# A grouped cosine transform on TensorE: from 64x64 tiles in two turns to sixteen 32x32 tiles, placed in front of the side work

## The chip, the core and the metric

The kernel runs on one core of a Trainium2 chip. A core has a matrix engine (TensorE, PE in the profile, its weight loads shown apart as PEld), VectorE (DVE), ScalarE (ACT), GpSimd (POOL), and SyncE (SP), which here only issues DMAs. Each engine works through its own instructions in order; semaphores tie them together. DMA engines, sixteen for this core, move data between device memory and the on-chip memory of 128 partitions. TensorE writes into PSUM, eight banks of 2 KB per partition.

The metric is the device time of one execution in microseconds (us). Three runs of the kernel before gave 6804.09, 6806.48 and 6808.73 us.

## What is computed

Layer 0 is a block-matching network on x of shape (8, 32, 128, 128), normalised per group; layer 1 is a 5x5 convolution. Cut to what matters:

```python
xb = _patch_match_stack(x)            # for each pixel the 8 best offsets: 32*8 = 256 channels, c*8 + k
dct = _conv(xb, dct_w, groups=C)      # 1x1, 32 groups of 8 channels -> 8 channels each
h = relu(_conv(_conv(xb, w1), w2, groups=CK, pad=1))
h = relu(_conv(_conv(h, w3), w4, groups=CK, pad=1))
wiener = sigmoid(_conv(_conv(h, w5), w6, groups=CK, pad=1))
filt = _conv(wiener * dct, inv_dct_w, groups=C)
x = x + _conv(filt, agg_w)            # layer 0, on the normalised x
x = x + _conv5x5(_gn(x), kernel)      # layer 1
```

The change concerns the second line, the cosine transform: a 256x256 matrix that is zero outside 32 blocks of 8x8.

## The kernel before, in words

An image is worked through in 16 row blocks of 8 rows (`NS`), and one more step that flushes the last rows: 17 steps for each of 8 images, 136 in all. The main loop runs over these steps and one slot for each stage, `i` in (3, 2, 1, 0), the stages being skewed against each other. In slots 3, 2 and 1 a 1x1 convolution (`pointwise_v` L649, `pointwise_t` L673) and a depthwise 3x3 run: half the channels on DVE in nine taps (`depthwise_v`, L703, the first tap on ACT at L700), half on PE (`depthwise_t`, L729). Every slot also gathers pixels for a later row block by one-hot matmuls (`gather_pixels`, L611, tile pg). Slot 0 finishes a row block: `final_dct` multiplies the network's output acc by the cosine transform, and in the next slot `final_add` (L809, L817) mixes down to 32 channels.

What other images need (patch distances, top-8, layer 1 of the previous image) is side work: generators that queue pieces for DVE ("D"), ACT ("A") and PE ("P" and "Q"), taken up by `run` at fixed places in each slot. Pieces of "P" are transposes (px, pt, pi), small statistics (pm, pv_a, pv_b) and the 5x5 convolution (two tiles p, L902). The order on PE, DVE and ACT is the program's order; DMAs are issued from POOL and SP.

PSUM: almost all matmul results go through one pool of five banks (`ps_x`): pv, p, pg, pc, pa, px, pt, pi and the rest. A new tile gets a bank once its earlier tile has been read by ACT or DVE. Two further banks belong to the depthwise stage, one to the patch distances.

The transform's way through memory: pixels are gathered into xb (partition 32j + c, second index g, for channel c*8 + 4g + j), which serves as input of the first convolution and is written to device memory as xbd by one DMA for each row block (L620), in the same layout. A step later `final_load` (L769) reads rows shifted by 3 back as xf, eight DMAs of 32 partitions. xf has a single buffer, so its next load waits for the matmuls that read it. `final_dct` then runs twice, for four rows each: two tiles pc (one for each half of the channels), four 64x64 matmuls of fp32 with up to 512 columns into them, and two DVE products L796. The weights ldct are built once in `mixes`: 32 small DMAs on SP into dq (L291), one reduction and two products on DVE.

In slot 0 the order on PE is: side work "P", final_dct, side work "Q", then pg.

Of the kernel before, what the change touches and what calls it, by code (L numbers as in the profile page):

```python
# [8 lines left out]
F32 = mybir.dt.float32  # L9
# [6 lines left out]
P = 128  # L16
C, K, H, W = 32, 8, 128, 128
CK = C * K
NO = 25
R = 8  # L20
# [14 lines left out]
C_M32 = C_G2 + 32  # L35
# [7 lines left out]
def bm3d_conv_preact(  # L43
# [16 lines left out]
    nc = tc.nc  # L60
    NB = x.shape[0]

    const = ctx.enter_context(tc.tile_pool(name="const", bufs=1))
    keep = ctx.enter_context(tc.tile_pool(name="keep", bufs=1))
    xnp = ctx.enter_context(tc.tile_pool(name="xn", bufs=1))
    work = ctx.enter_context(tc.tile_pool(name="work", bufs=2))
    dram = ctx.enter_context(
        tc.tile_pool(name="dram", bufs=2, space=bass.MemoryType.DRAM)
    )
    ps_x = ctx.enter_context(  # L70
        tc.tile_pool(name="ps_x", bufs=5, space=bass.MemoryType.PSUM)
    )
# [23 lines left out]
    cst = const.tile([P, C_N], F32, name="cst")  # L96
# [5 lines left out]
    lw5 = const.tile([P, 2, CK], F32, name="lw5")  # L102


    ldct = const.tile([P, 2, 64], F32, name="ldct")
    lagg = const.tile([P, 2, C], F32, name="lagg")


# [92 lines left out]
    def run(which, credit=1e9):  # L201

        q, took = queues[which], 0.0
        for _ in range(len(q) if which != "D" else 1000):

            i = next(
                (
                    i
                    for i, (c, _, at) in enumerate(q)
                    if at <= now[0] and (c != PAIR or pairs[0] < 2)  # L210
                ),
                None,
            )
            if i is None or took >= credit:
                break
            cost, task, _ = q[i]
            del q[i]
            took += cost
            pairs[0] += cost == PAIR
            push(task)  # L220
        if which == "Q":
            pairs[0] = 0
        return took
# [58 lines left out]

    def mixes():

        dq = work.tile([P, 2, K], F32, name="dq", tag="dq", bufs=1)
        src = dct_w.rearrange("(m h c i) k a b -> m h k c (i a b)", m=2, h=2, i=K)
        for k in range(K):
            for m in range(2):
                for h in range(2):
                    p = 64 * h + 8 * k  # L290
                    nc.sync.dma_start(dq[p : p + 8, m], src[m, (h + m + 1) % 2, k])  # L291
        m8 = work.tile([P, 8], F32, name="m8", tag="m16", bufs=1)
        yield "D", 1.0, 10
        nc.vector.tensor_reduce(
            m8,
            cst[:, C_M32 : C_M32 + C].rearrange("p (a c) -> p c a", c=8),
            axis=mybir.AxisListType.X,
            op=ALU.add,
        )
        for m in range(2):  # L300
            nc.vector.tensor_tensor(
                ldct[:, m].rearrange("p (c i) -> p c i", i=K),
                m8.unsqueeze(2).to_broadcast([P, 8, K]),
                dq[:, m].unsqueeze(1).to_broadcast([P, 8, K]),
                ALU.mult,
            )

        iv = work.tile([P, 2, K], F32, name="iv", tag="iv", bufs=1)
        nc.sync.dma_start(iv, inv_w.rearrange("(m p) k a b -> p m (k a b)", p=P))
        ag = work.tile([C, CK], F32, name="ag", tag="xr")  # L310
        nc.sync.dma_start(ag, agg_w.rearrange("c i a b -> c (i a b)"))
        for m in range(2):
            yield "D", 0.5
            ib = work.tile([P, P], F32, name=f"ib_{m}", tag="xm")
            nc.vector.tensor_tensor(
                ib.rearrange("p (c k) -> p c k", k=K),
                cst[:, C_M16 : C_M16 + 16].unsqueeze(2).to_broadcast([P, 16, K]),
                iv[:, m].unsqueeze(1).to_broadcast([P, 16, K]),
                ALU.mult,
            )  # L320
            yield "P", 0
            ps = ps_x.tile([P, 512], F32, name=f"ps_ag_{m}", tag="x")[:, :C]
            nc.tensor.transpose(ps, ag[:, m * P : (m + 1) * P], ident[:C, :C])
            agt = work.tile([P, C], F32, name=f"agt_{m}", tag="agt")
            nc.scalar.copy(agt, ps)
            yield "P", 0
            ps2 = ps_x.tile([P, 512], F32, name=f"ps_ia_{m}", tag="x")[:, :C]
            nc.tensor.matmul(ps2, ib, agt, start=True, stop=True)
            nc.scalar.copy(lagg[:, m], ps2)
# [270 lines left out]
    def gather_pixels(b, s4, g):  # L600

        n, h = s4 // 2, s4 % 2
        if h == 0 and g == 0:
            xbs[b, n] = xbp.tile([P, 2, R, W], F32, name=f"xb_{b}_{n}", tag="xb")
        xb, xt = xbs[b, n], xts[b, s4]
        sels = [selss.pop((b, s4, g, k2)) for k2 in range(2)]
        pg = ps_x.tile([P, 4, W], F32, name=f"pg_{b}_{s4}_{g}", tag="x")
        for t in range(NT):
            xa, xz = TW * t, min(TW * (t + 1), W)
            for j in range(4):  # L610
                nc.tensor.matmul(  # L611
                    pg[C * j : C * (j + 1), :, xa:xz],
                    xt[:, t],
                    sels[j // 2][:, j % 2, :, xa:xz],
                    start=True,
                    stop=True,
                )
        nc.scalar.copy(xb[:, g, 4 * h : 4 * h + 4], pg)
        if h == 1 and g == 1:
            nc.gpsimd.dma_start(xbd[b][:, :, R * n : R * (n + 1)], xb)  # L620

# [124 lines left out]
    def final_load(b, n):  # L748
        j0, j1 = (3, R) if n == 0 else (0, R if n < NS else 3)
        ya, yz = R * n - 3 + j0, R * n - 3 + j1  # L750

        whole = j1 - j0 == R
        nr, nw = (2, W) if whole else (j1 - j0, C)
        xr = work.tile([P, 2 * W], F32, name=f"xr_{b}_{n}", tag="xr")
        xr = xr[:, : nr * nw].rearrange("p (r w) -> p r w", w=nw)
        for j in range(4):
            ra = ya + 2 * j if whole else ya
            xa = 0 if whole else C * j
            nc.gpsimd.dma_start(
                xr[C * j : C * (j + 1)], x[b, :, ra : ra + nr, xa : xa + nw]  # L760
            )

        xf = xbp.tile([P, 2, R, W], F32, name=f"xf_{b}_{n}", tag="xf", bufs=1)
        src = xbd[b].rearrange("(j m h c) g y x -> g m h j c y x", j=4, m=2, h=2)
        for m in range(2):
            for h in range(2):
                for g in range(2):
                    p = 64 * h + C * g
                    nc.gpsimd.dma_start(  # L769
                        xf[p : p + C, m, j0:j1], src[g, m, (h + m + 1) % 2, :, :, ya:yz]  # L770
                    )
        return xr, xf, j0, j1

    def final_dct(b, n, acc, xf, j0, j1):

        for r0 in range(0, R, 4):
            a, z = max(r0, j0), min(r0 + 4, j1)
            if a >= z:
                continue


            pc = [
                ps_x.tile([P, 4, W], F32, name=f"pc_{b}_{n}_{m}_{r0}", tag="x") for m in range(2)
            ]
            for h in range(2):
                for m in range(2):
                    o = 64 * ((h + m + 1) % 2)
                    nc.tensor.matmul(  # L788
                        pc[m][o : o + 64, : z - a],
                        ldct[64 * h : 64 * h + 64, m],  # L790
                        xf[64 * h : 64 * h + 64, m, a:z],
                        start=True,
                        stop=True,
                    )
            for m in range(2):
                nc.vector.tensor_mul(acc[m][:, a:z], acc[m][:, a:z], pc[m][:, : z - a])  # L796

    def final_add(b, n, acc, xr, j0, j1):

# [213 lines left out]
    with tc.manual_schedule(engines=ORDERED):  # L1013
        push(prep(0))
        push(weights())
        push(mixes())
        xbd[0] = dram.tile([P, 2, H, W], F32, name="xbd_0", tag="xbd")
        for i in range(3):
            nc.gpsimd.memset(tb[i][0:64, :, 0], 0.0)
        for u in range(7):  # L1020
# [12 lines left out]
        for s in range(len(steps) + 2):  # L1033
            if s < len(steps):
                b, n = steps[s]
                if s == 2:
                    push(bands())
                if n == (0 if b else 4) and b + 1 < NB:
                    until(lambda: b in ready, 4.0)
                    push(prep(b + 1))  # L1040
                if n == NS - 1 and b + 1 < NB:
                    until(lambda: b + 1 in ready, 4.0)
                    xbd[b + 1] = dram.tile([P, 2, H, W], F32, name=f"xbd_{b+1}", tag="xbd")
            for i in (3, 2, 1, 0):
                si = s - (i - 1 if i else 2)
                live = 0 <= si < len(steps)
# [10 lines left out]
                if live and not i:  # L1057
# [1 line left out]
                        x1d[bi] = dram.tile([C, H, W], F32, name=f"x1d_{bi}", tag="x1d")  # L1059
                        stats[bi] = work.tile([P, NS + 1, 6], F32, name=f"stat_{bi}", tag="stat")  # L1060
                    xr, xf, j0, j1 = fins.pop(si)
                run("P")
                if live and not i:
                    final_dct(bi, ni, accs[3, bi, ni], xf, j0, j1)

                run("Q")
                if s < len(steps):
                    unit(gather_select, u + 1, (0,))
# [87 lines left out]
```

## Time and profile before

| | |
|---|---|
| median of 3 runs | 6806.48 us |
| span of the profiled execution | 6807.3 us |
| mean granted TensorE clock | 0.973 |
| pc matmuls, L788 | 2112 records, median 589 ns |
| products L796 on DVE | 528, median 681 ns |
| idle of PE and its weight loads ahead of pc, until DVE's L796 | 93.6 us |
| idle of DVE until PE's pc | 59.8 us |
| xf loads on POOL, L769 | 1088 issues, 650.2 us busy; median 7.1 us to landing |
| xbd writes on POOL, L620 | 128 issues, median 732 ns |
| dq loads on SP, L291 | 32 issues, 661 to 870 ns |

The span is that of one execution taken by the hardware profiler. A line of a view by groups gives line, engine, operation, result<-inputs with shapes, count, then busy time and mean duration, then idle time of the engine just before, with what ended it (the releaser). In the view by time each row is a start, a duration, and the merged instructions of one kind; a bracket gives the idle time before it. The records of a matmul overlap: one of 512 columns lasts 589 ns, but tiles side by side start a few ns apart and the next round starts when the array is free. An fp32 matmul has two records.

### The profile page before, as it was taken

The numbers are of one execution on the slowest core, as the hardware profiler recorded it, in microseconds if no ns is written. First come the engines' busy times: TensorE is split into PE (matmuls) and PEld (weight loads), VectorE is DVE, ScalarE is ACT, GpSimd is POOL, SyncE is SP. The second block draws the span as 40 slices with busy tenths as digits, with TensorE's granted clock in tenths as the row PEclk, the third lists the DMA queues.
The fourth block names the chain that finished last, engine by engine and source line by source line (L and its number), as shares of the span: only waits on it lengthen the run. The fifth ranks groups of instructions, "written<-read, shape, count | busy, mean of one in ns | idle before, by whom it ended". The sixth has DMA issues, their size and how long they took to land.

```text
span 6807.3 us, 257036 instructions
## 1 busy us (share of the span) xinstructions
PE 6354.3 (93%) x113378; PEld 3352.8 (49%) x113378; DVE 5860.4 (86%) x8822; ACT 5064.6 (74%) x6698; POOL 3246.7 (48%) x5351
## 2 busy tenths in 40 slices
PE   5798899999999999999999999999999999999997
PEld 1454454554545455454554455545555454455553
DVE  7789988989889898898988888899888899877776
ACT  5787778777687777877777777877769777687772
POOL 7354446444464444544445444454436554344334
PEclk8899999999999999999999999999999999999998
DMA  4566656666566675666756656566665666566653
GB/s 90 143 153 153 151 149 154 159 152 158 147 156 155 144 169 135 163 151 152 167 135 158 161 146 169 138 165 159 149 150 151 162 156 152 138 170 157 154 151 80
DMA packets 809627, 1021.41 MB, mean 150 GB/s; under 512 B 255456, under 2 KB 619936, under 8 KB 808512
## 3 DMA queue, kind: packets, MB, share of 16 engines
q0 software_dynamic: 422432, 745.61, 42.9%
q1 hardware_dynamic: 383568, 258.11, 17.4%
q8 instruction: 892, 14.61, 0.9%
q10 hardware_dynamic: 2512, 1.25, 0.1%
q14 instruction: 223, 1.83, 0.1%
HBM read 553.25 MB, written 217.01 MB: 113 GB/s over the span
## 4 chain that ended last, share of the span: by engine, by line
PE 55%; DVE 23%; ACT 8%; DMA 6%; issue 5%; POOL 3%; SPq 0%; ACTq 0%; DVEq 0%; POOLq 0%
PE pw L729 18%; DVE acc L703 15%; PE pv L649 13%; PE p L673 12%; PE pg L611 4%; DVE df L421 3%; PE pc L788 2%; DMA t<-t 2%; PE p L902 2%; ACT df L429 2%; ACT ib L596 2%; DVE idx L514 1%; PE pa L809 1%; DMA xf<-xbd 1%; DVE acc L796 1%
## 5 line engine op out<-in xcount | busy, mean ns | idle before, releaser
L703 DVE SCALAR_TENSOR_TENSOR acc<-tv,dwv,acc 128x1024 f32<-128x1024 f32 (+3 forms) x3264 | 4032.9, 1237 | 249.6 <-ACT acc L700 140.3
L729 PE MATMUL pw<-t,dwd 96*32 96x254 f32 (+7 forms) x31680 | 2144.1, 422 | 84.7 <-issue 40.5
L729 PEld LDWEIGHTS pw<-t,dwd 96*32 96x32 f32 (+1 forms) x31680 | 1103.9, 111 | 906.6 <-issue 440.7
L582 POOL DMA_DIRECT2D ib<-idxd x1024 | 570.7, 558 | 1796.5 <-ACT sel L597 1620.6
L596 ACT ACTIVATE ib<-ib,nplace 128x1024 bf16<-128x1024 bf16 x1024 | 1170.1, 1143 | 9.5 <-DMA ib<-idxd 9.5
L597 ACT ACTIVATE sel<-ib 128x1024 f32<-128x1024 bf16 x1024 | 1084.8, 1059 | 32.5
L673 PE MATMUL p<-acc,lw 128*32 128x256 f32 x16768 | 989.1, 381 | 25.3 <-ACT tv L657 22.7
L649 PE MATMUL pv<-acc,lw 128*128 128x512 f32 (+1 forms) x2112 | 980.7, 607 | 29.9 <-DVE acc L796 27.4
L769 POOL DMA_DIRECT2D xf<-xbd x1088 | 650.2, 630 | 304.2 <-PE pc L788 87.0
L673 PEld LDWEIGHTS p<-acc,lw 128*32 128x32 f32 x16768 | 556.2, 111 | 454.9 <-ACT tv L657 62.5
L657 ACT COPY tv<-pv 128x512 f32<-128x512 f32 (+2 forms) x784 | 438.1, 578 | 390.4 <-PE pv L649 374.2
L611 PEld LDWEIGHTS pg<-sel,xt 128*32 128x32 f32 x45056 | 575.5, 111 | 252.1 <-issue 54.2
L429 ACT ACTIVATE df<-df 128x786 f32<-128x786 f32 (+2 forms) x576 | 468.0, 859 | 291.9 <-DVE df L421 289.2
L611 PE MATMUL pg<-sel,xt 128*32 128x48 f32 x45056 | 592.7, 207 | 80.4 <-ACT sel L597 46.0
L421 DVE TENSOR_TENSOR df<-xn 128x786 f32<-128x786 f32 (+2 forms) x576 | 532.5, 976 | 116.0 <-PE pd L436 109.2
L742 ACT ACTIVATE acc<-pw 128x512 f32<-128x512 f32 (+2 forms) x808 | 439.9, 573 | 249.7 <-PE pw L729 249.0
L649 PEld LDWEIGHTS pv<-acc,lw 128*128 128x128 f32 x2112 | 384.2, 193 | 475.6 <-issue 398.1
L707 ACT ACTIVATE acc<-acc 128x1024 f32<-128x1024 f32 (+3 forms) x408 | 416.8, 1022 | 229.7 <-DVE acc L703 229.5
L680 ACT COPY t<-p 128x512 f32<-128x512 f32 x800 | 424.6, 570 | 127.7 <-PE p L673 125.7
L700 ACT ACTIVATE acc<-tv,dwv 128x1024 f32<-128x1024 f32 (+3 forms) x408 | 454.5, 1114 | 52.6 <-PE pa L809 35.0
L649 PE MATMUL pv<-xb,lw 128*128 128x512 f32 x1024 | 477.4, 609 | 0.0
L673 PE MATMUL p<-xb,lw 128*32 128x256 f32 x8192 | 468.1, 380 | 4.4 <-DVE xy L914 4.4
(151 smaller groups left out, 5782.5 us busy)
## 6 DMA issues: line engine op xcount, KB each, us to landing
ib<-idxd POOLq DMA_DIRECT2D x1024, 256.0 KB, 4.4
xbd<-xb POOLq DMA_DIRECT2D x128, 1024.0 KB, 6.7
xf<-xbd POOLq DMA_DIRECT2D x960, 128.0 KB, 7.3
t<-t SPq DMA_DIRECT2D x792, 128.0 KB
t<-t SPq DMA_DIRECT2D x384, 256.0 KB
tv<-tv SPq DMA_DIRECT2D x384, 130.0 KB
xt<-xtd POOLq DMA_DIRECT2D x240, 176.0 KB, 4.6
xl<-xs POOLq DMA_DIRECT2D x256, 64.0 KB, 2.6
```

Source lines behind the costliest of these rows:

```text
L421: nc.vector.tensor_sub(df[:, :, ca:cz], xn[:, r0 : r0 + SR, ca:cz], xn[:, r0 + dy : r0 + dy + SR, ca + dx : cz + dx],)
L429: nc.scalar.activation(df[:, :, ca:cz], df[:, :, ca:cz], AF.Square)
L582: nc.gpsimd.dma_start(ib.rearrange("p k y x -> p (k y x)"), idxd[b][s4 // 8, s4 % 8, 4 * k0 : 4 * k0 + 8] .rearrange("k x -> (k x)") .part ...
L596: nc.scalar.activation(ib, ib, AF.Square, bias=nplace)
L597: nc.scalar.activation(sel, ib, AF.Relu, scale=-1.0, bias=1.0)
L611: nc.tensor.matmul(pg[C * j : C * (j + 1), :, xa:xz], xt[:, t], sels[j // 2][:, j % 2, :, xa:xz], start=True, stop=True,)
L649: nc.tensor.matmul(ps[:, :hr], lhsT[:, g, P:CK], src(g)[:, h : h + hr], start=g == 0, stop=g == 1,)
L673: nc.tensor.matmul(ps[C * r : C * (r + 1), e, :nb], lhsT[:, g, s], rows[:, r : r + 4 * nb - 3 : 4], start=g == 0, stop=g == 1,)
L700: nc.scalar.activation(acc, rows, AF.Copy, scale=tap)
L703: nc.vector.scalar_tensor_tensor(acc, rows, tap, acc, op0=ALU.mult, op1=ALU.add)
L729: nc.tensor.matmul(pt[u][C * j : C * (j + 1), ka:kz, :nb, xa:xz], dwd[0:hi, i - 1, u, j, dx + 1], t[0:hi, j, ka:kz, :nb, xa + dx : xz + dx ...
L769: nc.gpsimd.dma_start(xf[p : p + C, m, j0:j1], src[g, m, (h + m + 1) % 2, :, :, ya:yz])
```

## The change

The transform is cut into 32x32 tiles. The channels go to xbd in natural order (c*8 + k), so that 32 consecutive channels are four whole blocks of 8; xbd is written by four DMAs in place of one. xf is loaded for s = 0 to 3 (channel half s // 2, rows 4 (s % 2) and on) with the partitions rotated by 32 s, in one or two DMAs each: seven for a full step instead of eight. `final_dct` takes four pc tiles at once and issues sixteen 32x32 matmuls: row group q of the array writes column group (q + s) % 4 of tile s, so that all sixteen lie on different tiles of the array. Then come four products. ldct has four parts instead of two, dq is loaded by 64 DMAs instead of 32, and DVE does four products in `mixes` instead of two. In the main loop final_dct moves ahead of `run("P")`.

```diff
-        for k in range(K):
-            for m in range(2):
-                for h in range(2):
-                    p = 64 * h + 8 * k
-                    nc.sync.dma_start(dq[p : p + 8, m], src[m, (h + m + 1) % 2, k])
+        src = dct_w.rearrange("(m q c i) k a b -> m q c k (i a b)", m=2, q=4, i=K)
+        for s in range(4):
+            for q in range(4):
+                for c in range(4):
+                    p = C * q + K * c
+                    nc.sync.dma_start(dq[p : p + K, s], src[s // 2, (q + s) % 4, c])
...
-            nc.gpsimd.dma_start(xbd[b][:, :, R * n : R * (n + 1)], xb)
+            for j in range(4):
+                nc.gpsimd.dma_start(
+                    xbd[b].rearrange("(c g j) y x -> j c g y x", g=2, j=4)[
+                        j, :, :, R * n : R * (n + 1)
+                    ],
+                    xb[C * j : C * (j + 1)],
+                )
...
-        for m in range(2):
-            for h in range(2):
-                for g in range(2):
-                    p = 64 * h + C * g
+        src = xbd[b].rearrange("(m p) y x -> m p y x", m=2)
+        for s in range(4):
+            m, r0 = s // 2, s % 2 * 4
+            a, z = max(r0, j0), min(r0 + 4, j1)
+            for pa, pz, at in ((0, P - C * s, C * s), (P - C * s, P, 0)):
+                if a < z and pa < pz:
                     nc.gpsimd.dma_start(
-                        xf[p : p + C, m, j0:j1], src[g, m, (h + m + 1) % 2, :, :, ya:yz]
+                        xf[pa:pz, m, a:z],
+                        src[m, at : at + pz - pa, R * n - 3 + a : R * n - 3 + z],
                     )
...
+        parts = [(s, max(s % 2 * 4, j0), min(s % 2 * 4 + 4, j1)) for s in range(4)]
+        parts = [(s, a, z) for s, a, z in parts if a < z]
+        pc = {
+            s: ps_x.tile([P, 4, W], F32, name=f"pc_{b}_{n}_{s}", tag="x") for s, a, z in parts
+        }
+        for q in range(4):
+            for s, a, z in parts:
+                o = C * ((q + s) % 4)
+                nc.tensor.matmul(
+                    pc[s][o : o + C, : z - a],
+                    ldct[C * q : C * (q + 1), s],
+                    xf[C * q : C * (q + 1), s // 2, a:z],
+                    start=True,
+                    stop=True,
+                )
+        for s, a, z in parts:
+            m = s // 2
+            nc.vector.tensor_mul(acc[m][:, a:z], acc[m][:, a:z], pc[s][:, : z - a])
...
-                run("P")
                 if live and not i:
                     final_dct(bi, ni, accs[3, bi, ni], xf, j0, j1)
-
+                run("P")
                 run("Q")
```

More of the change, by code (lines that the diff above doesn't have):

```diff
@@ L102, in bm3d_conv_preact @@
     lw5 = const.tile([P, 2, CK], F32, name="lw5")
-    ldct = const.tile([P, 2, 64], F32, name="ldct")
+    ldct = const.tile([P, 4, C], F32, name="ldct")
     lagg = const.tile([P, 2, C], F32, name="lagg")
@@ L283, in mixes @@
     def mixes():
-        dq = work.tile([P, 2, K], F32, name="dq", tag="dq", bufs=1)
-        src = dct_w.rearrange("(m h c i) k a b -> m h k c (i a b)", m=2, h=2, i=K)
-        for k in range(K):
-            for m in range(2):
-                for h in range(2):
-                    p = 64 * h + 8 * k
-                    nc.sync.dma_start(dq[p : p + 8, m], src[m, (h + m + 1) % 2, k])
-        m8 = work.tile([P, 8], F32, name="m8", tag="m16", bufs=1)
+        dq = work.tile([P, 4, K], F32, name="dq", tag="dq", bufs=1)
+        src = dct_w.rearrange("(m q c i) k a b -> m q c k (i a b)", m=2, q=4, i=K)
[4 more added lines that the diff above has]
+                    nc.sync.dma_start(dq[p : p + K, s], src[s // 2, (q + s) % 4, c])
+        m4 = work.tile([P, 4], F32, name="m4", tag="m16", bufs=1)
         yield "D", 1.0, 10
         nc.vector.tensor_reduce(
-            m8,
-            cst[:, C_M32 : C_M32 + C].rearrange("p (a c) -> p c a", c=8),
+            m4,
+            cst[:, C_M32 : C_M32 + C].rearrange("p (a c) -> p a c", a=4),
             axis=mybir.AxisListType.X,
@@ L299, in mixes @@
         )
-        for m in range(2):
+        for s in range(4):
             nc.vector.tensor_tensor(
-                ldct[:, m].rearrange("p (c i) -> p c i", i=K),
-                m8.unsqueeze(2).to_broadcast([P, 8, K]),
-                dq[:, m].unsqueeze(1).to_broadcast([P, 8, K]),
+                ldct[:, s].rearrange("p (c i) -> p c i", i=K),
+                m4.unsqueeze(2).to_broadcast([P, 4, K]),
+                dq[:, s].unsqueeze(1).to_broadcast([P, 4, K]),
                 ALU.mult,
@@ L763, in final_load @@
         xf = xbp.tile([P, 2, R, W], F32, name=f"xf_{b}_{n}", tag="xf", bufs=1)
-        src = xbd[b].rearrange("(j m h c) g y x -> g m h j c y x", j=4, m=2, h=2)
-        for m in range(2):
-            for h in range(2):
-                for g in range(2):
-                    p = 64 * h + C * g
+        src = xbd[b].rearrange("(m p) y x -> m p y x", m=2)
+        for s in range(4):
+            m, r0 = s // 2, s % 2 * 4
+            a, z = max(r0, j0), min(r0 + 4, j1)
+            for pa, pz, at in ((0, P - C * s, C * s), (P - C * s, P, 0)):
+                if a < z and pa < pz:
                     nc.gpsimd.dma_start(
-                        xf[p : p + C, m, j0:j1], src[g, m, (h + m + 1) % 2, :, :, ya:yz]
+                        xf[pa:pz, m, a:z],
+                        src[m, at : at + pz - pa, R * n - 3 + a : R * n - 3 + z],
                     )
@@ L774, in final_dct @@
     def final_dct(b, n, acc, xf, j0, j1):
[L776 to L796, printed above, removed]
+        parts = [(s, max(s % 2 * 4, j0), min(s % 2 * 4 + 4, j1)) for s in range(4)]
[16 more added lines that the diff above has]
+            nc.vector.tensor_mul(acc[m][:, a:z], acc[m][:, a:z], pc[s][:, : z - a])
     def final_add(b, n, acc, xr, j0, j1):
@@ L1016, in bm3d_conv_preact @@
         push(mixes())
-        xbd[0] = dram.tile([P, 2, H, W], F32, name="xbd_0", tag="xbd")
+        xbd[0] = dram.tile([CK, H, W], F32, name="xbd_0", tag="xbd")
         for i in range(3):
@@ L1042, in bm3d_conv_preact @@
                     until(lambda: b + 1 in ready, 4.0)
-                    xbd[b + 1] = dram.tile([P, 2, H, W], F32, name=f"xbd_{b+1}", tag="xbd")
+                    xbd[b + 1] = dram.tile([CK, H, W], F32, name=f"xbd_{b+1}", tag="xbd")
             for i in (3, 2, 1, 0):
```

## The prediction, made before the changed kernel was run

> **What bounds the kernel now.** I read the page's parts first: engine shares, then the chain that ended last.
>
> ```profile
> PE 6354.3 (93%) x113378; PEld 3352.8 (49%) x113378; DVE 5860.4 (86%) x8822; ACT 5064.6 (74%) x6698; POOL 3246.7 (48%) x5351
> ...
> PE 55%; DVE 23%; ACT 8%; DMA 6%; issue 5%; POOL 3%; SPq 0%; ACTq 0%; DVEq 0%; POOLq 0%
> ```
>
> TensorE bounds more than half of the span, VectorE about a quarter, and they take turns: stretches in which PE never idles alternate with stretches in which the nine-tap depthwise on DVE (L703) ends last. So a saving on PE counts in the first kind and vanishes in the second. The whole chain, piece by piece, holds 165 us of "PE pc L788" (the page rounds to 2%). I went through the 136 groups of pc (one per row step) in order of time. 92 stand without side work just before them; in 56 of those the chain runs through the whole group (1.88 us). In the others the chain is on DVE.
>
> A plain group, PE's rows in order of time (start, duration, engine, line, operation, count):
>
> ```profile
> 3054.75 1.06 PE L729 MATMUL pw<-t,dwd 128*32 128x508 f32 x8
> 3055.74 1.95 PE L788 MATMUL pc<-xf,ldct 64*64 64x512 f32 x16
> 3057.62 1.12 PE L611 MATMUL pg<-sel,xt 128*32 128x48 f32 x88
> ```
>
> Eight matmuls are 16 records, two passes each. Single records start in fours 7 ns apart, and the fours 0.43 us apart: four rounds of 0.43 plus about 0.17 at the ends is 1.88 us until pg.
>
> A group behind the 5x5 convolution's p (L902), PE and DVE:
>
> ```profile
> 3097.07 10.52 DVE L703 SCALAR_TENSOR_TENSOR acc<-tv,dwv,acc 128x1024 f32<-128x1024 f32 x8
> ...
> 3103.68 4.48 PE L902 MATMUL p<-xm,band 64*64 64x512 f32 x40
> ...
> 3107.98 2.97 PE L788 MATMUL pc<-xf,ldct 64*64 64x512 f32 x16
> ...
> 3109.13 1.28 DVE L796 TENSOR_TENSOR acc<-acc,pc 128x512 f32<-128x512 f32 x2 [1.53 <-PE pc L788]
> 3109.87 0.20 PEld L788 LDWEIGHTS pc<-xf,ldct 64*64 64x64 f32 x6 [0.89 <-DVE acc L796]
> 3110.89 1.01 PEld L611 LDWEIGHTS pg<-sel,xt 128*32 128x32 f32 x88 [0.81 <-DVE acc L796]
> ```
>
> The two p tiles hold two of the five PSUM banks, so the fourth pc waits for the first multiply to give its bank back. From the first p to pg PE needs 7.21 us. DVE's taps end at 3107.59: it is free 3.91 us after p begins.
>
> **1. Sixteen 32x32 tiles.** Two rounds instead of four: 2 x 0.43 + 0.17 + twelve more tiles at 7 ns (0.08) = 1.11 to 1.14 us, a saving of 0.74. No row of this trace has over four tiles at once, so this is the change's largest unknown; the ends are below. Two rules of the Trainium skill bear on it. "TensorE: Matmul & The Clock Gate" (Part 3, what overlaps and what doesn't) says matmuls start in strict program order. In that order a tile's second pass would hold back the next tile's first: eight matmuls would take nine rounds, 3.9 us, and sixteen 17 rounds, 7.3 us. The trace has four rounds, and in the group above one tile's second pass ran while the next tile still waited for DVE, so both passes stand together in the program and the array takes other tiles past a waiting one. "TensorEngine Tiling (Array Packing)" (Gotcha 1) speaks against the change directly: different row tiles can't access one PSUM bank at the same time. Here all four row groups write every pc tile. By that rule they run one after another: 4 x 2 rounds = 3.4 us, 1.7 us worse per group. But today's pc has two row groups writing each bank and runs at full rate, so I take the row, not the rule. Between: a window that passes few waiting tiles gives three rounds (1.45 us, saves 0.43) or five (2.31 us, costs 0.43). I take two rounds, because nothing in the four-tile rows shows a limit. Sum: 56 x 0.74 = 41 us; some stretches will hand part to DVE, so **-38**.
>
> **2. pc in front of the side work.** Four pc tiles are now taken at once, then the side work asks for banks.
> - Behind p5 (the L902 rows; 13 groups, all on the chain): p needs two banks and one is free. Its second tile waits until the first multiply ends: DVE is free at 3.91, plus 0.68 is 4.59, plus 0.07 to wake PE. Then ten rounds less what ran, 4.3 us: pg at 8.97 instead of 7.21. DVE gains its 1.53 and 0.58 of waiting, but PE is the bound there (the next rows wait for PE). 13 x 1.76 = **+23**.
> - First step of an image with px and pv_b (6 groups on the chain): PE stands 6.29 us for the first multiply, then pays pc 1.98, pd 2.7, pg.
>
> ```profile
> 1134.51 1.29 PE L788 MATMUL pc<-xf,ldct 64*64 64x128 f32 x10
> 1142.09 1.98 PE L788 MATMUL pc<-xf,ldct 64*64 64x512 f32 x6 [6.29 <-DVE acc L796]
> ```
>
>   All pc now run before DVE arrives; what waits for the multiply's bank is at worst pv_b (0.28). Saves 1.7 each: **-10**; up to 6 each if pv_b gets another bank.
> - pi+pi (7 groups, in 5 the multiplies come 10.2 us after pi) and pt (8): the next tile takes either the bank of the side tile, freed by an ACT copy within about 1.5 us, or pc's, freed by DVE. With the first, 0. With the second, pg waits for the multiply and pv comes 1.1 + 5.2 us after it instead of at once: 5 x 6.3 = 31 us for pi. For pt ACT's later copy of pv covers it (17.9 us after pt, pv's end by then at most 16). I take **0** and keep 31 as an end; below zero there is nothing, as the multiplies themselves end no earlier.
>
> **3. Setup.** SP's rows and DVE's rows of the setup:
>
> ```profile
> 23.42 22.99 SPq L291 DMA_DIRECT2D dq<-in_L_conv_dct_w_dram  x32
> ...
> 53.24 0.40 DVE L301 TENSOR_TENSOR ldct<-m,dq 128x64 f32<-128x64 f32 x2
> ```
>
> 64 issues of 64 four-byte elements instead of 32: 23.0 us more of SP, dq complete at about 71.5 instead of 48. Today the 6.8 us until 53.24 hide it; then DVE, in order, would stand 18.3 us at L301, with the squares of the first image behind it (iv, ag and kb, queued after dq on SP, arrive by 73 and are not later than that). DVE idles 6.07 us at 78.88 today and is 97% busy in the 30 us after; the delay left there is 72.8 + 18.3 - 78.9 = **+12** (ends 6 and 18). It passes through idxd to the first gather, which starts the pipeline.
>
> **4. POOL and DMA.** xf: 7 issues for 8 (3 for 8 in an image's last step), at 0.6 us; xbd: 4 for 1, about 0.65 each: +1.3 us of POOL per step. POOL is 48% busy and waits 1620.6 us for sel before its ib loads, which cover this; ib waits of ACT are 9.5 us in all. Where dsum or x1d stand behind them: **+4** (0 to 10). xf's packets shrink from 4096 to 2048 bytes: the same DMA kinds took 188 and 98 ns (medians over the trace), 4% more per byte; xf lands a step ahead. Nothing. Two more DVE products at 0.2 us in the setup: nothing.
>
> **Sum** against the profiled run (span 6807.3 us, 0.8 above the 6806.48 median, so the two are interchangeable): -38 + 23 - 10 + 0 + 12 + 4 = -9, **6797 us**, within 0.2% (14 us, about what a measurement tells from no change).
>
> **Rivals.**
> - A (45%): as above, gain and new waits nearly cancel. Own range 6772 to 6822.
> - B (25%): the array doesn't hold sixteen tiles. For it: nothing in the trace exceeds four, and the tiling rule. Against: today's two row groups. Five rounds turn -38 into +25: 6860. Three rounds: 6813. It decides at four rounds.
> - C (18%): banks. After pi the pool hands out pc's bank, and PE stands behind DVE's late multiplies: +31, 6828. For it: PE's 93.6 us of idle at pc already ends on L796. It decides as soon as pi or pg has a wait released by L796 of over 5 us.
> - D (12%): better than A. The gain counts in all plain groups (92 x 0.74 = 68) and pv_b runs early (36): 6807 - 68 - 36 + 23 + 12 = 6738. For it: DVE's waits for pc (59.8 us) go. Against: with DVE late, pv waits for L796 whatever PE does.
>
> **How the numbers follow.** Slower than 6820: all of five rounds (15%), three rounds in half (7%), most of C (16%), A's upper tail (7%): 45%. Faster than 6793: D and A's lower tail, 30%. Between: 25%. The range 6748 to 6860 leaves about 1 in 10 at each end.
>
> **What will show it.** pc x32 records in about 1.2 us, in two rounds (A) or more (B). pg or pi waiting for L796 (C). p of L902 waiting some 3.5 us for L796 in 13 groups. DVE idle 18 us ahead of ldct in the setup, and the first pc 12 us later. I am wrong if pc's group isn't near 1.1 us, if the L902 waits are absent, or if the DVE stretches shift as a whole.

## The result, and the profile after

The changed kernel took 6881.02 us (median of 4 runs, 6877.89 to 6884.7); the kernel before, beside it on the same chip, 6807.6. The ratio is 1.0102, 95% interval 1.0088 to 1.0115: 73 us slower, where 6797 was forecast. A second set of runs on another chip gave 6877.38 against 6801.93, ratio 1.0112 (1.0092 to 1.0132).

The page of the changed kernel, engine shares and the chain that ended last:

```profile
PE 6305.0 (92%) x115490; PEld 3350.9 (49%) x115490; DVE 5861.2 (85%) x8824; ACT 5060.9 (74%) x6698; POOL 3264.3 (47%) x5567
...
PE 44%; DVE 31%; issue 7%; ACT 7%; DMA 7%; POOL 3%; SPq 0%; ACTq 0%; DVEq 0%; POOLq 0%
```

TensorE is busy 49 us less than before, as a smaller transform should make it, and its share of the chain has fallen by 11 points. The time was not saved: it turned into waits. The view of waits, PE alone (us in all, times, longest):

```profile
PE pw L735 <- DMA t<-t: 80.0, 21, 11.1
...
PE pg L611 <- DVE acc L801: 39.4, 10, 7.0
PE pv_b L248 <- DVE acc L801: 39.2, 6, 6.6
PE p L907 <- DVE acc L801: 35.6, 13, 3.5
```

The rows of the same view before:

```profile
PE pc L788 <- DVE acc L796: 38.3, 7, 6.4
...
PE pw L729 <- DMA t<-t: 27.5, 19, 4.4
```

Before, pg waited 3.0 us once for the products, and pv_b and p not at all; the 38.3 us of pc are gone after. (Lines move by a few between kernels: the products are L796 before, L801 here, L805 to L810 in the experiments; the 5x5 part's p is L902, L907, L911.)

Where did the time go? Each row step has four groups of pg; take the start of the first of them in both traces and subtract. Between steps 4 and 5 of images 1 to 6 the difference jumps by 12.2, 12.5, 11.9, 11.1, 10.7 and 11.1 us, and not in image 7. Over every other step it moves by at most 7.4 us, up or down: after the jumps of images 4 and 6 it falls by 7, and over steps 9 to 11, where the 5x5 part stands, it mostly rises. One of these places, PE of the changed kernel in order of time:

```profile
1203.94 2.75 PE L735 MATMUL pw<-t,dwd 96*32 96x256 f32 x46
1217.82 4.52 PE L735 MATMUL pw<-t,dwd 96*32 96x256 f32 x48 [11.13 <-DMA t<-t]
```

Before, the same 94 matmuls ran in one go:

```profile
1195.68 5.33 PE L729 MATMUL pw<-t,dwd 96*32 96x256 f32 x94
```

The second half of pw needs rows of t that SP's queue copies from one group of partitions to another. SP's rows, first before, then after:

```profile
1185.03 0.50 SPq L635 DMA_DIRECT2D tv<-tv  x1
1187.27 0.59 SPq L685 DMA_DIRECT2D t<-t  x1
1187.90 0.94 SPq L687 DMA_DIRECT2D t<-t  x1
1192.25 0.59 SPq L628 DMA_DIRECT2D t<-t  x1
1197.23 0.50 SPq L635 DMA_DIRECT2D tv<-tv  x1
```

```profile
1193.28 12.75 SPq L641 DMA_DIRECT2D tv<-tv  x2
1206.12 0.63 SPq L634 DMA_DIRECT2D t<-t  x1
1206.85 1.10 SPq L691 DMA_DIRECT2D t<-t  x1
1208.00 1.41 SPq L693 DMA_DIRECT2D t<-t  x1
```

Before, the shift of t (L685, L687) goes out between two copies of tv. After, the second tv<-tv stands in front of it, and SP waits 11.67 us in the middle of "x2" for DVE's taps to have read the rows that it overwrites. PE runs out of work at 1206.69. The two parts of the shift go out at 1206.85 and 1208.00, and the second, the one for which PE waits longest, lands 9.7 us after its issue. It lands among other traffic. The next answer gives for a stretch how long PE, PEld, DVE, ACT and POOL were busy, then the granted clock, the busy share of the DMA engines and GB/s; in its first row the DMA engines are 92% busy, with a row block's stores of xbd and its loads of xf.

```profile
1206.00:1218.00 12.00, 0.87 (x18) 0.40 (x12) 11.57 (x34) 3.68 (x5) 5.88 (x11) 0.71 0.92 272
1218.00:1230.00 12.00, 12.00 (x104) 5.15 (x103) 6.36 (x12) 5.24 (x7) 0.00 (x0) 0.86 0.08 20
```

Nothing in the diff writes this order down. `manual_schedule` takes the program's order for PE, DVE and ACT only; SP and POOL are ordered when the program is planned, and the plan came out differently. The orders of the two programs differ in several places; the swap shown, the copy of tv ahead of the shift of t in step 3 of stage 1, stands in images 1 to 6 and in no other: the images with the jumps.

### The profile page after: what moved, and what is told of

The parts are those of the page before. It is cut to its first block, busy times and chain, and to the rows that moved or that the text cites. A ratio compares the mean times of both kernels' runs of the same rounds, so it can differ in the third digit from the quotient of the medians.

```text
span 6876.1 us, 261554 instructions
## 1 busy us (share of the span) xinstructions
PE 6305.0 (92%) x115490; PEld 3350.9 (49%) x115490; DVE 5861.2 (85%) x8824; ACT 5060.9 (74%) x6698; POOL 3264.3 (47%) x5567
## 4 chain that ended last, share of the span: by engine, by line
PE 44%; DVE 31%; issue 7%; ACT 7%; DMA 7%; POOL 3%; SPq 0%; ACTq 0%; DVEq 0%; POOLq 0%
DVE acc L709 23%; PE pw L735 15%; PE pv L655 12%; PE p L679 9%; PE pg L611 3%; DMA t<-t 3%; DVE df L421 2%; PE p L907 2%; DVE idx L514 2%; ACT ib L596 1%; PE pa L814 1%; ACT df L429 1%; ACT acc L706 1%; PE pd L436 1%; DVE acc L801 1%
## 5 line engine op out<-in xcount | busy, mean ns | idle before, releaser
L735 PE MATMUL pw<-t,dwd 96*32 96x254 f32 (+7 forms) x31680 | 2178.3, 427 | 127.7 <-DMA t<-t 80.0
L735 PEld LDWEIGHTS pw<-t,dwd 96*32 96x32 f32 (+1 forms) x31680 | 1129.7, 112 | 959.0 <-issue 510.1
L596 ACT ACTIVATE ib<-ib,nplace 128x1024 bf16<-128x1024 bf16 x1024 | 1169.8, 1142 | 10.1 <-DMA ib<-idxd 10.1
L776 POOL DMA_DIRECT2D xf<-xbd x920 | 488.6, 545 | 243.6 <-PE pc L792 52.9
L618 ACT COPY xb<-pg 128x512 f32<-128x512 f32 x512 | 300.3, 587 | 240.8 <-PE pg L611 235.6
```

Source lines behind the costliest of these rows:

```text
L596: nc.scalar.activation(ib, ib, AF.Square, bias=nplace)
L735: nc.tensor.matmul(pt[u][C * j : C * (j + 1), ka:kz, :nb, xa:xz], dwd[0:hi, i - 1, u, j, dx + 1], t[0:hi, j, ka:kz, :nb, xa + dx : xz + dx ...
L776: nc.gpsimd.dma_start(xf[pa:pz, m, a:z], src[m, at : at + pz - pa, R * n - 3 + a : R * n - 3 + z],)
```

## The experiments

Two theories. **Queue**: the six swaps cost most of the 73 us. **Contention**: the new stores and loads slow all transfers, and the swaps are only where it shows. And, for what is left, the forecast's own terms: what do the tiles give, and what does the move in front of the side work cost? Each kernel ran beside runs of the kernel before on its chip; those spread from 6779 to 6823 us, so a few us between two kernels tell nothing.

### One order restored: a_six

```diff
-            nc.sync.dma_start(t[0:64, :, 1], t[64:P, :, 2])
+            shift[i] = nc.sync.dma_start(t[0:64, :, 1], t[64:P, :, 2])
...
-            nc.sync.dma_start(v[:, 0:2], v[:, R : R + 2])
+            with tc.issue_after(shift[i].ins) if i == 1 and n == 3 and b else nullcontext():
+                nc.sync.dma_start(v[:, 0:2], v[:, R : R + 2])
```

> The changed kernel with one order restored: in row step 3 of images 1 to 6, the sync queue's copy of the two u rows of stage 1 (tv<-tv) is kept behind the two t<-t shifts of the same step, as it stood before the change; six places, nothing else. Queue theory (the planner put tv<-tv, which waits for VectorE's taps, in front of the t<-t shift that TensorE's second half of pw waits for): the jumps of 10.7 to 12.5 us between steps 4 and 5 of images 1 to 6, 69.5 in all, go; 6881 - 69.5 = 6811, 6800 to 6820. Contention theory (the four xbd stores and the 2 KB packets make the shifts land late, and the order is only where it shows): the jumps stay, 6870 to 6885.

6838.38 us, ratio 1.0048 (1.0032 to 1.0064). Up to step 4 of image 1 its trace follows the changed kernel's within some 3.5 us; then the 12.2 is 0.0. Of the six jumps of 69.5, two small ones stay (7.2 and 4.5 in images 2 and 6). The contention theory, as stated, is out; but the time fell by less than the sum of the jumps: the profiled spans differ by 45.4 us, the medians below by 39, and later steps had given some back (-3.2 right after the first).

### The changed kernel once more: after_again

> The changed kernel itself, beside the same runs of the kernel before, for the price of the six places: with them held it stood at 1.0048 of before. Queue theory: 1.0095 to 1.0115, so 32 to 46 us for six places.

6877.38 us, ratio 1.0112. Against a_six the six places are 39 us, over half of the loss.

### The bad order in the kernel before: b_broken

```diff
+            early = nc.sync.dma_start(v[:, 0:2], v[:, R : R + 2])
+            if i == 1 and n == 3 and b:   # the wide t<-t shift behind it, in order of issue only
+                tc.add_manual_dep(lead[i].ins, early.ins.name, ...)
```

> The kernel before, with the order of the changed kernel forced at the same six places (tv<-tv ahead of the wide t<-t shift of stage 1); nothing of the cosine transform is touched. Queue theory: + 6 x 11 to 12 = 6807 + 69 = 6876, 6860 to 6885. Contention theory: 6807 as before, since neither the stores nor the loads differ.

6837.59 us, ratio 1.0044 (1.0027 to 1.006): +36, not +69. With not a byte of the transform touched, the same waits appear, jumps of 7 to 10.9 us in the same six steps (two of them, in images 4 and 6, are followed by a fall of about 7). They are shorter than in the changed kernel; the longest row is:

```profile
1204.80 1.50 PE L740 MATMUL pw<-t,dwd 96*32 96x256 f32 x12 [7.14 <-DMA t<-t]
```

Order is the cause. That these waits are shorter is the edit's doing, for it does not copy the changed kernel's order in full. It puts only the wide part of the shift (L696) behind tv<-tv; the narrow part (L698) still goes out some 11 us before PE runs out of work, while in the changed kernel both stand behind. So the last part to go out in this row does so 2.4 us before PE runs out, and in the changed kernel's row above 1.3 us after: 3.7 of the 4.0 us. It lands 9.4 us after its issue here, 9.7 there, with the DMA engines 98% busy from 1196 to 1206 here too. In these two rows next to nothing is left for the new stores and loads.

### The move alone: b_front_six

The kernel before with these lines exchanged, and the six places held as in a_six:

```diff
-                run("P")
                 if live and not i:
                     final_dct(bi, ni, accs[3, bi, ni], xf, j0, j1)
+                run("P")
```

> The kernel before with its 64x64 transform called ahead of the side work, and the sync queue's order held at the six places: the move alone. Queue theory: the forecast's terms of the move stand as they are, p of the 5x5 part waits for the first multiply in 13 groups (+23 or, with the longer 64x64 group, a little more), the px and pv_b groups give 10 back: 6807 + 13 = 6820, 6812 to 6830. Rival (the move is what costs, through banks: pi and pg behind the multiplies): 6850 or more.

6863.44 us, ratio 1.0075 (1.0059 to 1.0092): not +13, but +51 by the ratio (61 by the medians). The rival has it. The three rows of waits for the products are there with 64x64 tiles too (pg 39.6 us in 10, pv_b 38.5 in 6, p 26.9 in 12).

### The tiles alone: a_behind_six

The exchange above undone in the changed kernel. Four pc at once and two tiles of the 5x5 part would be six banks of a pool of five, so pc is taken in pairs (the tiles are taken and the products made inside the loop over pairs too):

```diff
+        for pair in ([x for x in parts if x[0] % 2 == r] for r in range(2)):
-        for q in range(4):
-            for s, a, z in parts:
+            for q in range(4):
+                for s, a, z in pair:
```

> The changed kernel with its sixteen tiles called behind the side work as before the change, two banks at a time (four at once do not fit beside the 5x5 part's two), and the same six places held: the tiles, loads and stores alone. Queue theory: the plain groups give their 38 us, no new wait for p: 6807 - 38 = 6769, 6760 to 6785. Rival (the new loads and stores cost something of their own, or the tiles' gain is hidden): 6800 or more.

6792.5 us, ratio 0.9979 (0.9966 to 0.9991): 14 us faster, not 38. A miss. With pairs a plain group takes 1.27 us until pg, where it takes 1.08 with four at once and 1.88 before; over 56 groups these 0.19 us are 11 of the missing 24. PE's waits also grew, those of pc for products from 38.3 us to 48.2 and those of pw for t<-t from 27.5 to 35.4. What the rest is stays open.

### Half in front: a_half

Pair 0 ahead of `run("P")`, pair 1 behind it.

> The changed kernel with the six places held; of the transform only the two banks of rows 0 to 3 are written in front of the side work, the two of rows 4 to 7 behind it. Bank theory (what the move costs is that four of the pool's five banks wait for VectorE while the 5x5 part, pv_b, pt and then pg need one): with two banks held in front, p of the 5x5 part and pv_b find free banks, their waits for the products (36.5 us in 13 and 39.4 us in 6 with the whole transform in front) go, and the time comes near that with all of it behind: 6775 to 6805. Rival (the move costs because VectorE's or the queues' work around it shifts, not banks): half of it in front still costs half or more, 6815 to 6840.

6786.84 us, ratio 0.9979 (0.9967 to 0.9991). With two banks held instead of four, p and pv_b wait for no product, pg still does (23.0 us in 7), and against the tiles behind the side work in pairs (0.9979) nothing of the move's cost is left. Half of the products had moved all the same, so it is the number of banks held, and not the new place alone. In six places the later pc still waits 5.6 to 6.2 us for a product (36.6 us in all), as with 64x64 tiles before; "best" below removes those.

### The order of tv held everywhere: a_behind_full; tv issued by ScalarE: a_behind_actv

a_behind_full drops the condition of a_six. a_behind_actv has `nc.scalar.dma_start(v[:, 0:2], ...)` instead.

> The tiles behind the side work, with tv<-tv held behind the two t<-t shifts of its own stage and step everywhere, not only at the six places. Queue theory: 15 places more change order, in which the row of PE waiting for t<-t (35.4 us in 22) may fall by up to 20: 6755 to 6795, not slower than with six. Rival (elsewhere the shift of tv is the one that is needed first): slower than 6795.

> The tiles behind the side work, no place held, but the shift of the two u rows (tv<-tv) issued by ScalarE instead of the sync queue: there it stands behind ScalarE's own pass over acc, which follows the taps, so nothing behind it waits for VectorE. Queue theory: no t<-t shift can stand behind a tv<-tv, the waits of pw for t<-t fall from 35.4 us to below 25 and the time is at or below that of the six-place kernel: 6755 to 6795. Rival (ScalarE pays 384 issues of about 0.5 us, and gets late itself): 6800 to 6850.

6789.61 us, ratio 0.9975 (0.9963 to 0.9987): as with the six places alone. And 6808.74 us, ratio 1.0003 (0.9991 to 1.0015), with pw's waits for t<-t up from 35.4 to 57.2 us. The first lies in its range, but not for its reason: 15 more places held did not shorten pw's waits for t<-t (41.3 us). The second is a miss, and its rival has the time: freeing SP of the copy brought nothing. So no further cost of SP's order shows. Why issuing the copy from ScalarE costs 19 us more than a_behind_full, beside it on the same chip, was not followed up.

### A longer setup: a_dq2

All 64 loads of dq issued twice, the first time into a tile that nothing reads.

> The changed kernel with the six places held and the 64 loads of dq issued twice, first into a tile that nothing reads, so that dq is complete about 23 us later, at about 72 instead of 48 us. The forecast's third step (VectorE stands at ldct until dq is there, and the first gathers start later): VectorE's first product into ldct at about 73 instead of 53.6, and everything after it +12 (6 to 18): 6850. Rival (setup is not on the path at all): the first pg within 2 us of 142.

6853.0 us, one run. DVE stands where the forecast had it stand, first 3.12 us and then three times:

```profile
56.45 0.19 DVE L303 TENSOR_TENSOR ldct<-m,dq 128x32 f32<-128x32 f32 x1 [3.12 <-DMA dq<-in_L_conv_dct_w_dram]
61.67 0.19 DVE L303 TENSOR_TENSOR ldct<-m,dq 128x32 f32<-128x32 f32 x1 [5.03 <-DMA dq<-in_L_conv_dct_w_dram]
```

The four waits are 18.6 us, and the first pg comes at 159.7 instead of 142.1: +17.6, the upper end of the forecast's 6 to 18.

### Tiles behind, four banks when they are free: best

a_behind_full, with pairs only while a tile of the 5x5 part is open:

```diff
+        sets = [[x for x in parts if x[0] % 2 == r] for r in range(2)]
+        for pair in sets if five[0] else [parts]:
```

> The tiles behind the side work, tv<-tv held behind the t<-t shifts of its stage and step everywhere, and four banks at once again wherever no tile of the 5x5 part is open (two at a time only there). If the pairs are what keeps the gain small (a group's matmuls then start over 0.75 instead of 0.56 us: 0.19 x 56 plain groups = 11 us), 6778, 6765 to 6790, some 10 below the same kernel with pairs. Rival (the gain is lost in waits of the matrix engine that end on nothing the profile shows, and on t<-t): no difference from pairs, 6785 to 6795.

6752.96 us, ratio 0.9922 (0.9906 to 0.9938): 0.78% faster than before, and 37 us faster than with pairs, where 11 were expected. The expected reason is not the main one: most of it comes from six places, the step with px and pv_b in images 1 to 6. There PE of a_behind_full, then of best:

```profile
1962.02 1.96 PE L798 MATMUL pc<-xf,ldct 32*32 32x512 f32 x14 [6.50 <-DVE acc L807]
```

```profile
1944.83 0.49 PE L391 MATMUL px<-cst,xn 128*128 128x128 f32 x3
1945.16 0.28 PE L249 MATMUL pv_b<-tmp_b,cst 128*128 128x1 f32 x2
1945.37 1.05 PE L801 MATMUL pc<-xf,ldct 32*32 32x128 f32 x6
1947.78 1.79 PE L801 MATMUL pc<-xf,ldct 32*32 32x512 f32 x26 [1.36 <-ACT tmp_b L250]
```

With pairs (and with 64x64 tiles before) one of the later pc gets a bank that a product must free first, 5.9 to 6.5 us later. Asked for in one go, all four get banks that ACT frees, the last after 1.36 us. PE's waits of pc for products fall from 48.7 us to 10.1, and at the next step's pg the lead over a_behind_full has grown by 5.7 to 7.8 us, 39.7 in the six. In images 2, 4 and 5 the step after that gives 6.3 to 6.6 back, with a wait of pw for t<-t of 3.4 to 3.8 us in it; the two profiled executions differ by 25.2 us in all, and the one of best is the slowest of its six runs. Whether 64x64 tiles, asked for in one go, would have gained the same at these places was not run.

## Why the prediction was wrong, step by step

Chained by their medians (on three chips, where the kernel before had 6801.94, 6804.69 and 6801.93), the runs give: tiles behind the side work -49 (best), the move in front +85 (a_six against best), the six places +39 (after_again against a_six); together +75. The forecast had -38, +13 (23 and -10), +12 and +4. The -49 is not the -38 come true: with pairs the same tiles gave 14, and the rest came with the way the banks are asked for, which the forecast did not count there. That -49 lies near -38 is luck.

**1, two rounds: right; what they are worth (-38) was not shown.** A plain group in the changed kernel:

```profile
1200.34 1.15 PE L792 MATMUL pc<-xf,ldct 32*32 32x512 f32 x32
1201.42 0.88 PE L436 MATMUL pd<-df,neg 128*32 128x390 f32 x8
```

PE goes on 1.08 us after the first pc, where 1.11 to 1.14 was worked out and before it was 1.88. The forecast had weighed this row against the rule of the Trainium skill ("TensorEngine Tiling (Array Packing)", Gotcha 1) that row tiles can't write one bank at the same time, which by its estimate would have made 3.4 us; the measurement decides for the row. Rival B falls with it.

**2, the move: this is the term that failed first, +13 where the runs show +51 (with 64x64 tiles) to +85; none of its three lines held in full, and Rival C's mechanism came true at another place.**
- "13 x 1.76 = +23" for p. The wait came, in all 13 groups, and was even shorter than forecast (2.7 us on average, not 3.5). But from the first of p and pc to pg the 13 take 10.74 us on average, before 7.23: 3.5 each, 46. The forecast let the rest of p run at full clock after the wait. In three of the 13 groups it did, and these take 7.7 to 8.8 us, below the forecast's 8.97; eight have 3.4 us at half clock and take 10.4 to 11.7, two have 6.8 us of it and take 12.5 and 12.8. A group of a_six with 6.8:

```profile
1299.12 1.15 PE L796 MATMUL pc<-xf,ldct 32*32 32x512 f32 x32
1300.20 1.07 PE L911 MATMUL p<-xm,band 64*64 64x512 f32 x2
1304.34 7.21 PE L911 MATMUL p<-xm,band 64*64 64x512 f32 x38 [3.07 <-DVE acc L805]
```

 Forty records of p last 4.48 us before; here 38 take 7.21, with the granted clock at 0.50 from 1303.07 to 1309.89.
- "pi and pt 0." pi was nearly right: in a_six pg waits 0.4 us or less behind it in nearly all groups, and pi itself once 2.5. At pt, pg of a_six waited for the products in every image from 0 to 6, up to 6.6 us, and ACT's later copy did not cover it:

```profile
1518.58 1.94 PE L612 MATMUL pg<-sel,xt 128*32 128x48 f32 x88 [6.35 <-DVE acc L805]
```

- "-10" at px and pv_b, with "pv_b then waits at worst 0.28". It waited 6.4 to 6.6 us in each of 6: the bank wait went from pc to pv_b, and of the saving 0.4 to 1.0 us each was left at the next step's first pg, 4.6 in all. The saving with "up to 6 each" exists, but behind the side work, as best shows.

**3, setup: the mechanism was right, its size was not.** The forecast took before's 675 ns for each of 64 issues. SP's row now:

```profile
23.87 23.75 SPq L291 DMA_DIRECT2D dq<-in_L_conv_dct_w_dram  x64
```

At a median of 304 ns each, 64 issues take as long as 32 did, dq is complete when DVE arrives, and the first pg is 0.2 us later. a_dq2 shows that the +12, rather 18, would have come with twice the time.

**4, POOL and the DMA engines** could not be told apart from nothing in these runs.

**Missing: SP's order in the main loop.** The forecast counted what the change queues on SP in the setup and took the order of the main loop for given. That was 39 us.

## What to carry to other kernels

Before costing a reordering, count the buffers that the moved work holds and who frees them: four banks held until a late engine came made the tiles that asked next (p, pv_b, pg) wait for that engine, and asking for all four in one go behind the side work was worth more here (37 us against pairs) than the tiles in pairs alone (14 us). Where a queue's order is left to a planner, an edit elsewhere can change it; compare the issue order before and after, and pin the transfers that a busy engine is about to need ahead of those that wait for one. A wait on the matrix engine can cost more than its length, when the matmuls behind it run at half clock.

## What the hardware showed beyond that

- **The clock behind a wait.** PE of a_six around the wait of 6.35 us shown above, over at 1518.58, in stretches of 3.41 us (PE's busy time stands first, the granted clock third from the end):

```profile
1507.86:1511.27 3.41, 3.41 (x60) 0.96 (x52) 3.34 (x3) 2.22 (x4) 0.54 (x1) 1.00 0.49 106
1511.27:1514.69 3.42, 0.96 (x20) 0.42 (x4) 3.31 (x4) 2.40 (x3) 2.07 (x4) 1.00 0.49 150
1514.69:1518.10 3.41, 0.00 (x0) 0.00 (x0) 3.34 (x4) 0.20 (x1) 0.56 (x1) 0.50 0.86 209
1518.10:1521.52 3.42, 2.94 (x100) 2.30 (x104) 3.32 (x14) 0.58 (x1) 0.07 (x1) 0.50 0.09 30
1521.52:1524.93 3.41, 3.41 (x68) 1.92 (x64) 3.27 (x15) 2.03 (x3) 3.41 (x7) 1.00 0.64 141
```

 The group of pg behind it takes 1.94 us, elsewhere 1.09. The stretches are chosen so because every change of the granted clock in the traces of before, after, a_six and best lies within 0.02 us of a grid of 3.413 us. From 300 to 6700 us of the changed kernel the clock fell 67 times, each time behind a stretch in which PE was busy for at most 52%; it never stayed at full behind a stretch below 43%, and it came back only behind stretches of 87% or more. So a stretch about half idle was enough, and whether a wait of 2 to 3 us cost clock depended on how it lay on the grid: the fall at 1303.07 came 1.8 us into its wait. The Trainium skill ("TensorE: Matmul & The Clock Gate", Part 1) says that the clock halves after an idle window of about 3.4 us, counted by a window that runs freely, and comes back after as long a busy one. The window and its free running agree with these traces; that it has to be idle throughout does not.
- **The price of a DMA issue** depended on its source: 64 four-byte elements took 675 ns to issue when each lay in another 32 bytes of a 2 KB range, 304 ns when all lay in 256 bytes, into the same shape of target. Only these two patterns were seen, so which property decides is open.
